# Row sums of a graph-attention layer: neighbouring key tiles added up by accumulating transfers before the product

## The chip, the cores and the metric

The kernel runs on one core of one Trainium2 chip. The metric is the device time of one execution in microseconds (us), from start to end of the program on that core; the number to forecast is the median over runs. Lower is better. In the text PE is the matrix engine (TensorE), DVE is VectorE, ACT is ScalarE, POOL is GpSimd, and SP is the engine that issues the plain DMAs.

## What is computed

Two attention layers over a graph of N = 2048 nodes, D = 256 features, for a batch of B = 8. Both end in a residual add and a layer norm:

```python
# layer 0: H = 8 heads of dh = 32
x_proj = einsum('bnd,hdf->bhnf', x, W)
e = leaky_relu(e_src[..., :, None] + e_dst[..., None, :], 0.2)
e = e + softplus(beta) * log(prior + 1e-6)      # prior = adj
e = where(adj > 0, e, -inf)
h = softmax(e, axis=-1) @ x_proj                # per head
x = layernorm(x + concat_heads(h) @ W_out.T)
# layer 1: one head of 256
e = where(adj > 0, leaky_relu((x @ W1) @ (x @ W2).T, 0.2), -1e12)
x = layernorm(x + relu(softmax(e, axis=-1) @ (x @ W3)))
```

The change sits in layer 0. There the kernel never forms a softmax. It uses that exp(leaky_relu(u + v)) can be written as a row factor times exp(v) times max(c, r), where c depends on the query and r on the key. So for a key tile of 128 keys and all 2048 queries it forms s = max(c, r) * m, with m the transposed edge weights. Two sums over the keys follow: the numerator, s times (exp(v) * x_proj), and the row sum (the softmax's denominator), s times exp(v). Both are matrix products with s as the moving operand.

## The kernel before

**Layer 0, class `Gat`, one object per batch element.** `project` makes the projected values `v` (already multiplied by exp) and `re`, which holds for each key and head r (`re[:, 0]`) and exp(v) (`re[:, 1]`). For elements 1 to 7 both are parked in DRAM (`v_d`, `re_d`) and fetched again by `load`.

`step` does one key tile for two heads. An element has 64 steps: an outer loop over 4 pairs of heads (`hp`), an inner one over 16 key tiles (`jt`). One step

- fetches the key tile's edge weights, 1 MB, into `mt` (L177, two buffers, issued by SP);
- makes one `s` tile of 128 x 2048 float32 for each of the two heads on DVE (L301). `s` has four buffers, which is two steps' worth;
- multiplies on PE (L309): first eight products into `val` (the numerator), then eight into `den` (the row sums). For `den` the stationary operand is exp(v) of the key tile, broadcast to 32 columns, so that every one of 32 output rows holds the same sum. Both accumulate in PSUM over the 16 key tiles.

After the last key tile `finish` copies `val` and `den` out on ACT (L323, L325), takes the reciprocals by way of DRAM (`rc`, `rec_d`) and, after every second pair of heads, fetches them as a broadcast tile `rb` (L336) and scales the numerator (L338). `rb` lives in the two buffers of the tag "d". In elements 1 to 7 nothing else uses that tag; the setup in element 0 does.

**Layer 1, class `Dot`.** For each of 16 query tiles: scores on PE (`e`, L402), a leaky relu out of PSUM on ACT (`p`, L404), the mask and row minimum on DVE (L407), exp on ACT (L408), then transposes on PE (`pt`, L421) that ACT copies out (`pts`, L423), and the product `acc` (L437). The scores of the next query tile are computed inside the step of the present one.

**How the two are laid beside each other.** The instruction order on PE is the order of the program text (`manual_schedule` for PE); the other engines' order is worked out by the framework's scheduler, and each engine then executes in order. The main loop runs layer 1 of element b-1 and layer 0 of element b together: one `Gat` step after every fourth tile of `output`, one after every second tile of `turn`, and then, in each `Dot.step`, zero to two steps at each of the three places where `fill` is called:

```python
        dot.step(lambda k: layer_0((2, 1, 1)[k]))
        for i in range(NT - 2):
            dot.step(lambda k: layer_0((0, 2 - (i % 2 == 1), 2 - (i % 14 == 13))[k]))
```

Element 0's layer 0 runs alone at the start (with the projections of the other elements between its steps), element 7's layer 1 alone at the end.

Of the kernel before, what the change touches and what calls it, by code (L numbers as in the profile page):

```python
# [9 lines left out]
F32 = mybir.dt.float32  # L10
BF16 = mybir.dt.bfloat16
I32 = mybir.dt.int32
AF = mybir.ActivationFunctionType
ALU = mybir.AluOpType
# [4 lines left out]
P = 128  # L19
# [8 lines left out]
def kernel(  # L28
# [26 lines left out]
    nc = tc.nc  # L55
    B, N, D = x.shape
    H, _, DH = w_proj.shape
    NT = N // P
    KC = D // P
    BK = 512  # L60
    NB = N // BK
    HALF = N // 2
    HP = 2
    NP = H // HP
    IG = BK // P

    const = ctx.enter_context(tc.tile_pool(name="const", bufs=1))
    dram = ctx.enter_context(tc.tile_pool(name="dram", bufs=1, space=DRAM))
# [3 lines left out]
    small = ctx.enter_context(tc.tile_pool(name="small", bufs=3))  # L72
# [3 lines left out]
    def mm_tile(name):  # L76
        return ps.tile([P, BK], F32, tag="mm", name=name)

    def wide_tile(name, tag, bufs, dtype=F32):
        return wide.tile([P, N], dtype, tag=tag, name=name, bufs=bufs)  # L80
# [69 lines left out]
    pen_d = dram.tile([N, N], BF16, name="pen_d")  # L150
    c_d = dram.tile([B, H, N], F32, name="c_d")
    v_d = dram.tile([B, P, NT, D], F32, name="v_d")
    re_d = dram.tile([B, P, 2, NT, H], F32, name="re_d")
    rec_d = dram.tile([B, NP, 4, HALF], F32, name="rec_d")
    x1_d = dram.tile([B, N, D], F32, name="x1_d")

    def make_mt(jt):

        a = wide.tile([P, NT, P], I32, tag="d", name="adj_t", bufs=2)
        nc.sync.dma_start(a, adj[:, ts(jt, P)].rearrange("(t p) j -> p t j", p=P))  # L160
        m = wide.tile([P, NT, P], F32, tag="p", name="m", bufs=2)
        nc.vector.tensor_scalar(m, a, 0.0, None, ALU.max)
        nc.scalar.activation(m, m, AF.Ln, bias=eps_prior)
        nc.scalar.activation(m, m, AF.Exp, scale=beta_c)
        nc.vector.scalar_tensor_tensor(m, a, 0.0, m, ALU.is_gt, ALU.mult)
        mt = wide_tile("mt", "mt", 2)
        for g in range(NB):
            t = mm_tile("mtp")
            for k in range(IG):
                nc.tensor.transpose(t[:, ts(k, P)], m[:, g * IG + k, :], ident)  # L170
            nc.scalar.copy(mt[:, ts(g, BK)], t)
        nc.sync.dma_start(mt_d[ts(jt, P), :], mt)
        return mt

    def load_mt(jt):
        mt = wide_tile("mt", "mt", 2)
        nc.sync.dma_start(mt, mt_d[ts(jt, P), :])  # L177
        return mt
# [21 lines left out]
    def row_tile(name, bufs=4):  # L200
        return small.tile([P, D], F32, tag="row", name=name, bufs=bufs)


    class Gat:
# [8 lines left out]
        def project(self):  # L213


            b = self.b
            kept = "v" if b == 0 else ("h3", "x1t")[b % 2]
            self.v = v = whole.tile([P, NT, D], F32, tag=kept, name="v")
            ed = small.tile([P, NT, H], F32, name="ed", bufs=1)
            es = small.tile([P, H, NT], F32, name="es", bufs=1)  # L220
            xb = x[b].rearrange("(t p) d -> p t d", p=P)
            xrs, xts = [], []

            def turn(g):
                if g % 2 == 0:
                    xr = wide.tile([P, 2 * IG, D], F32, tag="p", name="xr", bufs=2)
                    nc.sync.dma_start(xr, xb[:, ts(g // 2, 2 * IG), :])
                    xrs.append(xr)
                xt = chunk.tile([P, KC, BK], F32, tag="ht", name="xt", bufs=3)
                for kc in range(KC):  # L230
                    t = mm_tile("tr")
                    for k in range(IG):
                        nc.tensor.transpose(t[:, ts(k, P)], xrs[-1][:, g % 2 * IG + k, ts(kc, P)], ident)
                    nc.scalar.copy(xt[:, kc, :], t)  # L234
                xts.append(xt)

            turn(0)
            for g in range(NB):
                if g + 1 < NB:
                    turn(g + 1)  # L240
                for k in range(IG):
                    it = g * IG + k
                    t = mm_tile("proj")
                    for kc in range(KC):
                        nc.tensor.matmul(t[:, 0:D + 2 * H], xts[g][:, kc, ts(k, P)], wp[:, kc, :],  # L245
                                         start=(kc == 0), stop=(kc == KC - 1))
                    nc.scalar.copy(v[:, it, :], t[:, 0:D])
                    nc.scalar.copy(ed[:, it, :], t[:, D:D + H])
                    nc.scalar.copy(es[:, :, it], t[:, D + H:D + 2 * H])
                yield  # L250
            top = small.tile([P, 2, H], F32, name="top", bufs=1)
            nc.vector.tensor_reduce(top[:, 0, :], ed.rearrange("p t h -> p h t"), AX.X, ALU.max)
            nc.gpsimd.partition_all_reduce(top[:, 1, :], top[:, 0, :], P, bass_isa.ReduceOp.max)
            nc.vector.tensor_tensor(es, es, top[:, 1, :].unsqueeze(2).to_broadcast([P, H, NT]), ALU.add)
            nc.vector.tensor_tensor(ed, ed, top[:, 1:2, :].to_broadcast([P, NT, H]), ALU.subtract)
            self.re = re = small.tile([P, 2, NT, H], F32, name="re", bufs=2)
            nc.scalar.activation(re[:, 0], ed, AF.Exp, scale=-(1.0 - ALPHA))
            nc.scalar.activation(re[:, 1], ed, AF.Exp)
            v4 = v.rearrange("p t (h f) -> p (t h) f", f=DH)
            nc.vector.tensor_tensor(v4, v4, re[:, 1].rearrange("p t h -> p (t h)").unsqueeze(2).to_broadcast(  # L260
                [P, NT * H, DH]), ALU.mult)
            if b > 0:
                nc.sync.dma_start(v_d[b], v)
                nc.sync.dma_start(re_d[b], re)
            yield
            t = mm_tile("est")
            nc.tensor.transpose(t[:, 0:P], es.rearrange("p h t -> p (h t)"), ident)
            est = row_tile("est")[:, 0:P]
            nc.scalar.activation(est, t[:, 0:P], AF.Exp, scale=1.0 - ALPHA)
            nc.sync.dma_start(c_d[b].rearrange("h (t p) -> (h t) p", p=P), est)  # L270
            yield

        def load(self):
            self.v = whole.tile([P, NT, D], F32, name="v")
            nc.sync.dma_start(self.v, v_d[self.b])
            self.re = small.tile([P, 2, NT, H], F32, name="re", bufs=2)
            nc.sync.dma_start(self.re, re_d[self.b])

        def query_rows(self, h):
# [5 lines left out]
        def step(self, count=1):  # L285

            for _ in range(count):
                hp, jt = next(self.units)
                if jt == 0:
                    self.cs = [self.query_rows(hp * HP + a) for a in range(HP)]  # L290
                    self.val = pacc.tile([P, HALF], F32, tag="val", name="val")
                    self.den = pacc.tile([P, HALF], F32, tag="den", name="den")
                first = self.b == 0 and hp == 0
                while first and len(self.mts) < min(jt + 2, NT):
                    self.mts.append(make_mt(len(self.mts)))
                mt = self.mts[jt] if first else load_mt(jt)
                s = []
                for a in range(HP):
                    h = hp * HP + a
                    sa = wide_tile("s", "s", 4)  # L300
                    nc.vector.scalar_tensor_tensor(sa, self.cs[a], self.re[:, 0, jt, h:h + 1], mt, ALU.max, ALU.mult)  # L301
                    s.append(sa)
                for dst in (self.val, self.den):
                    for c in range(HALF // BK):
                        for q in range(4):
                            h = hp * HP + q % 2
                            w = (self.v[:, jt, ts(h, DH)] if dst is self.val
                                 else self.re[:, 1, jt, h:h + 1].to_broadcast([P, DH]))
                            nc.tensor.matmul(dst[ts(q, DH), ts(c, BK)], w,  # L309
                                             s[q % 2][:, ds(q // 2 * HALF + c * BK, BK)],  # L310
                                             start=(jt == 0), stop=(jt == NT - 1))
                if jt == NT - 1:
                    self.finish(hp)

        def finish(self, hp):

# [202 lines left out]
```

## Time and profile before

| | |
|---|---|
| median of 3 runs | 4691.11 us (4690.69 to 4692.31) |
| the profiled execution | 4692.34 us, of which the span from first to last instruction is 4690.5 us |
| mean granted PE clock | 0.982 |
| ACT busy | 1678.8 us (36%) |
| POOL busy | 4.5 us, 14 instructions |
| bytes moved by DMA | 852.27 MB, mean 182 GB/s |

Busy time of the engines in three stretches of the span:

| stretch, us | PE | DVE | ACT | DMA share |
|---|---|---|---|---|
| 117 to 234 (element 0) | 92.62 of 117 | 93.45 | 66.77 | 0.79 |
| 936 to 1053 (layer 0 beside layer 1) | 117.00 of 117 | 79.04 | 39.40 | 0.51 |
| 4446 to 4563 (layer 1 alone) | 117.00 of 117 | 24.49 | 59.65 | 0.15 |

The DMA share is the mean busy share of the core's 16 DMA engines. An engine's idle time is put down to the one that released it.

### The profile page before, as it was taken

The numbers are of one execution on the slowest core, as the hardware profiler recorded it, in microseconds if no ns is written. First come the engines' busy times: TensorE is split into PE (matmuls) and PEld (weight loads), VectorE is DVE, ScalarE is ACT, GpSimd is POOL, SyncE is SP. The second block draws the span as 40 slices with busy tenths as digits, with TensorE's granted clock in tenths as the row PEclk, the third lists the DMA queues.
The fourth block names the chain that finished last, engine by engine and source line by source line (L and its number), as shares of the span: only waits on it lengthen the run. The fifth ranks groups of instructions, "written<-read, shape, count | busy, mean of one in ns | idle before, by whom it ended". The sixth has DMA issues, their size and how long they took to land.

```text
span 4690.5 us, 64746 instructions
## 1 busy us (share of the span) xinstructions
PE 4474.0 (95%) x27164; PEld 2280.4 (49%) x27164; DVE 3048.5 (65%) x2316; ACT 1678.8 (36%) x3683; POOL 4.5 (0%) x14
## 2 busy tenths in 40 slices
PE   6798799998999989998999989999999989999899
PEld 4443344444444444444444444445454444444566
DVE  5787676666666666666766666666766666666221
ACT  6522133333333333333333333333333343333555
POOL 0000000000000000000000000000000000000000
PEclk9999899999999999999999999999999999999999
DMA  7788854555555454555544455555545555544111
GB/s 220 264 298 329 294 201 156 179 176 201 181 180 179 171 181 171 178 180 190 189 175 163 173 202 175 176 177 187 183 162 176 179 189 185 177 165 153 61 48 44
DMA packets 252789, 852.27 MB, mean 182 GB/s; under 512 B 33616, under 2 KB 152400, under 8 KB 174928
## 3 DMA queue, kind: packets, MB, share of 16 engines
q1 hardware_dynamic: 252496, 848.13, 52.0%
q8 instruction: 213, 3.49, 0.3%
q14 instruction: 80, 0.66, 0.0%
HBM read 772.15 MB, written 75.37 MB: 181 GB/s over the span
## 4 chain that ended last, share of the span: by engine, by line
PE 86%; DMA 2%; ACT 1%; DVE 1%; issue 0%; SPq 0%; DVEq 0%
PE e L402 19%; PE acc L437 19%; PE val L309 18%; PE den L309 17%; PE pt L421 5%; PE y L351 3%; PE h3p L371 2%; PE h1p L391 2%; DMA rb<-rec_d 1%; PE tr L366 1%; DVE s L301 0%; DVE ht L338 0%; DMA mt<-mt_d 0%; PE proj L245 0%; DMA rec_d<-rc 0%
## 5 line engine op out<-in xcount | busy, mean ns | idle before, releaser
L301 DVE SCALAR_TENSOR_TENSOR s<-c,re,mt 128x2048 f32<-128x2048 f32 x1024 | 2350.2, 2347 | 441.5 <-PE den L309 375.4
L309 PE MATMUL val<-s,v 128*32 128x512 f32 x8192 | 1018.7, 603 | 54.4 <-DVE s L301 54.3
L309 PE MATMUL den<-s,re 128*32 128x512 f32 x8192 | 995.2, 594 | 0.0
L437 PE MATMUL acc<-h,pts 128*128 128x256 f32 x4096 | 951.7, 380 | 14.7 <-ACT pts L423 14.7
L402 PE MATMUL e<-x1t,h 128*128 128x512 f32 x2048 | 904.3, 594 | 0.0
L437 PEld LDWEIGHTS acc<-h,pts 128*128 128x128 f32 x4096 | 750.4, 191 | 103.2 <-ACT pts L423 16.6
L407 DVE CUSTOM_DVE_ANT_0 p<-p,pen 128x2048 f32<-128x2048 f32 x128 | 293.4, 2292 | 482.4 <-ACT p L404 482.4
L423 ACT COPY pts<-pt 128x512 f32<-128x512 f32 x512 | 298.0, 584 | 841.6 <-PE pt L421 841.3
L402 PEld LDWEIGHTS e<-x1t,h 128*128 128x128 f32 x2048 | 379.7, 190 | 450.2 <-issue 424.6
L309 PEld LDWEIGHTS den<-s,re 128*32 128x32 f32 x8192 | 272.2, 110 | 617.8 <-issue 617.8
L309 PEld LDWEIGHTS val<-s,v 128*32 128x32 f32 x8192 | 235.3, 110 | 651.2 <-issue 544.8
L404 ACT ACTIVATE p<-e 128x512 f32<-128x512 f32 x512 | 305.6, 597 | 543.6 <-PE e L402 543.6
L445 DVE TENSOR_TENSOR z<-z,x1r 128x256 f32<-128x256 f32 x128 | 54.4, 425 | 463.6 <-ACT z L444 458.0
L408 ACT ACTIVATE p<-p,neg 128x2048 f32<-128x2048 f32 x128 | 256.7, 2005 | 267.6 <-DVE neg L407 267.6
L421 PEld LDWEIGHTS pt<-ident,p 128*128 128x128 f32 x2048 | 238.1, 141 | 223.3 <-issue 189.8
L421 PE MATMUL pt<-ident,p 128*128 128x128 f32 x2048 | 318.5, 279 | 5.2 <-ACT p L408 5.2
L351 PE MATMUL y<-wot,ht 128*128 128x256 f32 x512 | 140.5, 425 | 85.1 <-DVE ht L338 84.3
L444 ACT ACTIVATE z<-acc,rec 128x256 f32<-128x256 f32 x128 | 60.9, 476 | 356.6 <-PE acc L437 356.6
L194 ACT ACTIVATE f<-mv,eps_ln 128x1 f32<-128x1 f32 x256 | 74.5, 291 | 294.9 <-DVE mv L192 294.6
L351 PEld LDWEIGHTS y<-wot,ht 128*128 128x128 f32 x512 | 103.7, 211 | 129.7 <-DVE ht L338 87.5
L371 PE MATMUL h3p<-w3s,x1t 128*128 128x256 f32 x512 | 133.5, 386 | 7.3 <-ACT x1t L367 7.3
L245 PE MATMUL proj<-wp,xt 128*128 128x272 f32 x512 | 126.1, 397 | 1.5 <-ACT xt L234 0.7
(76 smaller groups left out, 1797.4 us busy)
## 6 DMA issues: line engine op xcount, KB each, us to landing
mt<-mt_d SPq DMA_DIRECT2D x496, 1024.0 KB, 4.8
c<-c_d SPq DMA_DIRECT2D x64, 1024.0 KB, 5.9
pen<-pen_d SPq DMA_DIRECT2D x128, 512.0 KB, 3.3
xr<-in_x_dram SPq DMA_DIRECT2D x16, 1024.0 KB, 8.5
adj_t<-in_adj_dram SPq DMA_DIRECT2D x16, 1024.0 KB, 7.2
mt_d<-mt SPq DMA_DIRECT2D x16, 1024.0 KB, 5.7
adj_r<-in_adj_dram SPq DMA_DIRECT2D x16, 1024.0 KB, 8.1
rb<-rec_d SPq DMA_DIRECT2D x64, 256.0 KB, 4.8
```

The costliest lines, as they stand in the source:

```text
L245: nc.tensor.matmul(t[:, 0:D + 2 * H], xts[g][:, kc, ts(k, P)], wp[:, kc, :], start=(kc == 0), stop=(kc == KC - 1))
L301: nc.vector.scalar_tensor_tensor(sa, self.cs[a], self.re[:, 0, jt, h:h + 1], mt, ALU.max, ALU.mult)
L309: nc.tensor.matmul(dst[ts(q, DH), ts(c, BK)], w, s[q % 2][:, ds(q // 2 * HALF + c * BK, BK)], start=(jt == 0), stop=(jt == NT - 1))
L351: nc.tensor.matmul(y[:, 0:D], ht[:, ts(it, P)], wot[:, g, :], start=(g == 0), stop=(g == 1))
L371: nc.tensor.matmul(t[:, 0:D], x1t[:, kc, ts(it - 1, P)], w3s[:, kc, :], start=(kc == 0), stop=(kc == KC - 1))
L402: nc.tensor.matmul(t, self.h1[:, kc, ts(it % IG, P)], self.x1t[:, kc, ts(c, BK)], start=(kc == 0), stop=(kc == KC - 1))
L404: nc.scalar.activation(p[:, ts(c, BK)], t, AF.Prelu, alpha=ALPHA)
L407: nc.vector.tensor_tensor_reduce(p, p, pen, -1.0, FMAX, ALU.add, ALU.min, neg)
L408: nc.scalar.activation(p, p, AF.Exp, bias=neg, scale=-1.0, accum_out=den)
L421: nc.tensor.transpose(t[:, ts(k, P)], p[:, ts(g * IG + k, P)], ident)
L423: nc.scalar.copy(pt, t)
L437: nc.tensor.matmul(acc, now[:, ts(k, P)], self.h3[:, j, :], start=(j == 0), stop=(j == NT - 1))
```

## The change

For elements 1 to 7, and for four pairs of neighbouring key tiles of every head, (1, 2), (5, 6), (9, 10) and (13, 14), the row-sum products of the two tiles become one. The first tile's s is multiplied, key by key, by the ratio exp(v of the first) / exp(v of the second); the result `d` is a new tile in the tag "d". The second tile's s is then added onto `d` by a DMA that accumulates, issued from POOL. One set of eight products with the second tile's exp(v) as weights gives the row sums of both. It is placed after the products of the key tile that comes two later (three after the pair's first); for the last pair, after tile 15. The numerator's products stay as they are. The ratios are a third plane of `re`, made in `project`.

```diff
@@ -63,6 +63,7 @@
+    PAIRED = (1, 5, 9, 13)
@@ -150,7 +151,7 @@
-    re_d = dram.tile([B, P, 2, NT, H], F32, name="re_d")
+    re_d = dram.tile([B, P, 3, NT, H], F32, name="re_d")
@@ -253,9 +254,13 @@
-            self.re = re = small.tile([P, 2, NT, H], F32, name="re", bufs=2)
+            self.re = re = small.tile([P, 3, NT, H], F32, name="re", bufs=2)
             nc.scalar.activation(re[:, 0], ed, AF.Exp, scale=-(1.0 - ALPHA))
             nc.scalar.activation(re[:, 1], ed, AF.Exp)
+            for k, jt in enumerate(PAIRED):
+                nc.vector.tensor_tensor(ed[:, k, :], ed[:, jt, :], ed[:, jt + 1, :], ALU.subtract)
+            nc.vector.memset(re[:, 2], 0.0)
+            nc.scalar.activation(re[:, 2, 0:len(PAIRED)], ed[:, 0:len(PAIRED)], AF.Exp)
@@ -300,17 +305,32 @@
-                for dst in (self.val, self.den):
-                    for c in range(HALF // BK):
-                        for q in range(4):
-                            h = hp * HP + q % 2
-                            w = (self.v[:, jt, ts(h, DH)] if dst is self.val
-                                 else self.re[:, 1, jt, h:h + 1].to_broadcast([P, DH]))
-                            nc.tensor.matmul(dst[ts(q, DH), ts(c, BK)], w,
-                                             s[q % 2][:, ds(q // 2 * HALF + c * BK, BK)],
-                                             start=(jt == 0), stop=(jt == NT - 1))
+                v, e = self.v, self.re[:, 1]
+                heads = [hp * HP + a for a in range(HP)]
+                broadcast_e = [e[:, jt, h:h + 1].to_broadcast([P, DH]) for h in heads]
+                self.products(self.val, [v[:, jt, ts(h, DH)] for h in heads], s, jt == 0, jt == NT - 1)
+                if self.b > 0 and jt in PAIRED:
+                    k = PAIRED.index(jt)
+                    self.sums = [wide_tile("d", "d", 2) for _ in heads]
+                    for d, sa, h in zip(self.sums, s, heads):
+                        nc.scalar.activation(d, sa, AF.Copy, scale=self.re[:, 2, k, h:h + 1])
+                elif self.b > 0 and jt - 1 in PAIRED:
+                    for d, sa in zip(self.sums, s):
+                        nc.gpsimd.dma_start(d, sa, accum_op=ALU.add)
+                    self.sums_e = broadcast_e
+                else:
+                    self.products(self.den, broadcast_e, s, jt == 0, self.b == 0 and jt == NT - 1)
+                if self.b > 0 and (jt - 3 in PAIRED or jt == NT - 1):
+                    self.products(self.den, self.sums_e, self.sums, False, jt == NT - 1)
                 if jt == NT - 1:
                     self.finish(hp)
+
+        def products(self, dst, weights, s, start, stop):
+            for c in range(HALF // BK):
+                for q in range(4):
+                    nc.tensor.matmul(dst[ts(q, DH), ts(c, BK)], weights[q % 2],
+                                     s[q % 2][:, ds(q // 2 * HALF + c * BK, BK)],
+                                     start=start, stop=stop)
```

`load` takes the third plane of `re` with it in the same way.

More of the change, by code (lines that the diff above doesn't have):

```diff
@@ L275, in load @@
             nc.sync.dma_start(self.v, v_d[self.b])
-            self.re = small.tile([P, 2, NT, H], F32, name="re", bufs=2)
+            self.re = small.tile([P, 3, NT, H], F32, name="re", bufs=2)
             nc.sync.dma_start(self.re, re_d[self.b])
```

## The prediction

> **What bounds the kernel now.** I read the page's first part, then the chain that ended last, then the groups, and then one loop turn in the timeline.
>
> ```profile
> PE 4474.0 (95%) x27164; PEld 2280.4 (49%) x27164; DVE 3048.5 (65%) x2316; ACT 1678.8 (36%) x3683; POOL 4.5 (0%) x14
> ...
> PE 86%; DMA 2%; ACT 1%; DVE 1%; issue 0%; SPq 0%; DVEq 0%
> ...
> L301 DVE SCALAR_TENSOR_TENSOR s<-c,re,mt 128x2048 f32<-128x2048 f32 x1024 | 2350.2, 2347 | 441.5 <-PE den L309 375.4
> L309 PE MATMUL val<-s,v 128*32 128x512 f32 x8192 | 1018.7, 603 | 54.4 <-DVE s L301 54.3
> L309 PE MATMUL den<-s,re 128*32 128x512 f32 x8192 | 995.2, 594 | 0.0
> ...
> L408 ACT ACTIVATE p<-p,neg 128x2048 f32<-128x2048 f32 x128 | 256.7, 2005 | 267.6 <-DVE neg L407 267.6
> ...
> mt<-mt_d SPq DMA_DIRECT2D x496, 1024.0 KB, 4.8
> ```
>
> PE carries 86% of the chain and DVE 1%: the kernel is PE-bound. DVE, which makes `s`, is idle 375.4 us because PE has not yet released an `s` buffer; PE in turn waits only 54.3 us for `s`. So DVE runs two steps ahead, held by the four buffers. The timeline shows the rhythm:
>
> ```profile
> 2555.06 1.90 PE L309 MATMUL val<-s,v 128*32 128x512 f32 x16
> 2556.78 1.90 PE L309 MATMUL den<-s,re 128*32 128x512 f32 x16
> ...
> 2559.10 7.03 PE L402 MATMUL e<-x1t,h 128*128 128x512 f32 x16
> 2566.06 1.92 PE L309 MATMUL val<-s,v 128*32 128x512 f32 x16
> ```
>
> ```profile
> 2555.29 9.14 DVE L301 SCALAR_TENSOR_TENSOR s<-c,re,mt 128x2048 f32<-128x2048 f32 x4 [1.97 <-PE den L309]
> ```
>
> A set of `val` or `den` products takes 1.72 us (2555.06 to 2556.78; the matmuls overlap, so starts are subtracted; the trace counts 16 instructions for eight calls). Two steps of `s` cost DVE 9.14 us, 2.3 us a tile, and start right after a `den` ends.
>
> **What the Trainium skill says.** "DMA: Bandwidth & Descriptors", § SWDGE vs HWDGE vs iDMA: a transfer that accumulates must be issued from GpSimd, whose software writes its descriptors. § Anatomy of one DMA of the same page gives about 2 us of fixed cost; § Bandwidth gives 6.15 us for a plain 1 MB load issued from GpSimd. The trace before has no such transfer; SP's 1 MB load lands in 4.8 us. "Collectives: The Full Stack", § The bandwidth ceiling, puts a DMA reduction at half the rate of a copy, because each result needs two source reads; no run here shows it yet. "SBUF — State Buffer", § Who interferes with whom: a two-input VectorE instruction disturbs GpSimd's reads, not its writes, so L301 should not hold up the descriptors (inferred there; not in this trace). "ScalarE: Activation LUTs", § What ACT_TABLE_LOAD costs: an ACTIVATE with one pointer operand on 2048 elements takes about 1990 ns; L408 agrees with 2005.
>
> **The change, part by part.**
>
> *Removed.* 7 elements x 4 head pairs x 4 tile pairs = 112 times, one set of `den` products goes (two out, one in): 112 x 1.72 = 193 us of PE, all on the path.
>
> *ACT.* 224 scaled copies at 2.0 us, 450 us, take ACT from 36% to about 46%: no bound. But ACT is in order, and behind a copy may stand a `pts` or `h1` copy that PE needs next. `pts` copies come every 2.2 us with some 1.4 us to spare (copied at 2575.93 + 0.59, PE done with the preceding `acc` at about 2577.6), and the copies of one pair become ready 2.3 us apart, at DVE's pace. Most delays hide. I take 0.3 us a pair, 34 us, plus 20 us for places where `h1` stands behind (a quarter of the turns). Bounds: 0 and 112 x 2 = 224 us.
>
> *The accumulating transfers.* 224 of 1 MB. Their price T is the unknown. The trace's DMA share of 0.51 in a 117 us stretch at 179 GB/s gives 0.51 x 117 / 20.9 MB = 2.85 us of all engines per MB of plain load. Lower end: SBUF is quicker than DRAM, and twice the reads hide partly, 4.2 us. Twice the plain price is 5.7. Upper end: the page's 6.15 us plus another read of 2.85, 9.0. I take 7.0, near the middle of 5.7 and 9.0. All 16 engines then carry 224 x 7.0 = 1570 us more, about 40% of the 3800 us in which they run, on top of 50%.
>
> *The wait added.* The second tile's `s` buffers are now free only when the transfer has landed, not when PE is done. Call four steps A (scaled), B (accumulated), C, D. D's `s` goes into B's buffers. From B's first `s` to the next B's first `s` stand: about 1 us of descriptors (an estimate: half the fixed cost), 2 T for both heads' transfers, which share the engines, 1 us of landing, 2.9 us for one `mt` load interleaved, and four more `s` tiles (D's second one, both of A', the first of B'), 9.2 us. Sum 14.1 + 2 T + 1 us for the semaphore and the SP issue of `mt` = 15.1 + 2 T. Up to 3.5 us of L407 and layer norm work on DVE falls into the same loop when it can't use the gap; I take half, 1.7 us. With T = 7.0: 29.1, or 30.8 us.
>
> PE's own cadence for four steps: a turn of `Dot` is 26.4 us with three steps and 29.8 us with four (2540 to 2596), so four steps take 32.1, less 1.72 = 30.4 us. The loop is 0.4 us longer than PE, and since steps are bunched I take 0.8 us, 91 times (13 of 16 pairs in an element): 73 us. In `turn`, with a step every 5.9 us, four steps take 23.6 - 1.7 = 21.9 us while the loop takes 29.1: 7.2 us, two cycles x 7 elements: 101 us. Behind the waiting `s` on DVE stand L407 and the layer norm, with slack of over ten us; behind it on SP stands the next `mt`, which waits for that `s` and holds `pen` and `x1r` behind it.
>
> *Late ends.* Pair (13, 14) is used one step later, at tile 15: 2 T + 5 = 19 us against 19 to 22 us of cover (the `val` set of tile 14, 1.7, tile 15, 3.4, a stretch of `Dot` between them, 7.9, and DVE's lead over PE, 6 to 9 by the timeline); 0.5 us x 28 = 14 us.
>
> *The tag "d".* `rb` and `d` share two buffers. After the second head pair the chain from the `ht` copy to L338's end takes 25 us (2455.5 to 2480.5), during which the next pair's second `d` can't start: some 17 us late, of which the slack leaves 4 us, x 7 = 28 us. At an element's end two of the four `rb` loads, so far issued early, come late: 1.5 us x 8 = 12 us. PE is already idle there for 10 us.
>
> *`project`, `re`.* Four small subtractions, a memset, one exp at 0.3 us per element, a transfer half as large again, hidden under element 0's layer 0 but for the first: 1 us.
>
> **Sum.** -193 + 54 + 73 + 101 + 14 + 40 + 1 = +90 us on the profiled 4692.3 us: 4782 us. The median of the runs is 1 us below the profiled execution: 4781. I say 4780.
>
> **Rivals.**
> *Faster: the buffers come back in time.* If T is 4.5 us the loop is 24.1 to 25.8 us, well under 30.4. Then `Dot` costs nothing, `turn` 2.2 x 14 = 31 us, the rest about 65: -193 + 96 = -97, 4594 us. For it: DVE's 375 us of waiting for PE and half the DMA time are free. Against it: the transfer must read two tiles in little more than 1.5 times a plain load's time. It turns into a loss at about T = 5.9, where stalls of some 83 us in `turn` stand beside 109 elsewhere.
> *Much slower: the transfer is three plain loads or more.* At T = 9.0 the loop takes 34.8 us: 4.4 x 91 = 400, `turn` 11.2 x 14 = 157, the rest 150, sum +514: 5206 us. At T = 12, some 1200 us more than before. For it: no view shows the accumulate rate; against it: DMA engines would sit near full load.
> *Nothing moves:* gain and stalls cancel within 9 us, 4691.
> *Another order on ACT:* if the scheduler puts the scaled copies ahead of `pts` and they wait for `s`, PE pays up to 2 us a pair: +170 us over the forecast, inside the slow cases.
>
> **How the numbers follow.** Slower as forecast (T 6 to 8): 0.44, own range 4705 to 4990. Much slower: 0.14. Faster: 0.37, own range 4560 to 4680. No change: 0.05. A range for 8 in 10 must reach into both sides: 4575 (leaving the best of the faster case) to 5210 (leaving the worst of the slowest). A measurement of this kernel tells 0.2%, some 9 us, from no change: faster 0.37, same 0.05, slower 0.58.
>
> **What would show it.** In the changed profile: `den` with 8192 - 1792 = 6400 instructions (112 x 16 gone) and, if my reason holds, a large idle time ahead of L301 put down to the accumulating DMA, and PE waiting for `s` far above 54 us, most at tiles 4 and 8, in `turn`. The transfers' time to landing, for two at once, would be 15 us or more. If they land within 10 us, L301 keeps waiting for PE alone and the forecast is wrong towards 4600. If PE instead waits for `pts` or `h1`, it was ACT's order. A longer wait at L351 would show the `rb` buffers.

## The result: 4829.9 us, and the profile after

The changed kernel takes 4829.93 us (median; 4826.25 to 4832.87), against 4691.71 us for the kernel before on the same chip: a ratio of 1.0288, 95% interval 1.0271 to 1.0306. It is 138 us slower. The profiled execution took 4826.25 us, its span 4824.4.

The page of the changed kernel, in the same order as before: the engines, the DMA queues, the costliest groups, the DMA issues.

```profile
PE 4424.8 (92%) x25372; PEld 2263.8 (47%) x25372; DVE 3052.6 (63%) x2356; ACT 2086.7 (43%) x3915; POOL 197.9 (4%) x238
...
q1 hardware_dynamic: 252496, 849.05, 48.7%
q0 software_dynamic: 32256, 234.90, 25.4%
...
L306 DVE SCALAR_TENSOR_TENSOR s<-c,re,mt 128x2048 f32<-128x2048 f32 x1024 | 2356.8, 2347 | 713.9 <-DMA mt<-mt_d 229.5
L331 PE MATMUL val<-s,v 128*32 128x512 f32 x8192 | 1063.1, 612 | 115.1 <-DVE s L306 114.9
...
L331 PE MATMUL den<-s,re 128*32 128x512 f32 x4608 | 615.7, 606 | 0.0
...
L316 ACT ACTIVATE d<-s,re 128x2048 f32<-128x2048 f32 x224 | 444.9, 2001 | 289.0 <-PE den L331 261.6
...
L331 PE MATMUL den<-d,re 128*32 128x512 f32 x1792 | 271.8, 643 | 69.8 <-DMA d<-s 69.8
...
mt<-mt_d SPq DMA_DIRECT2D x496, 1024.0 KB, 6.3
d<-s POOLq DMA_DIRECT2D x224, 1024.0 KB, 11.8
c<-c_d SPq DMA_DIRECT2D x64, 1024.0 KB, 15.3
```

`den` has 4608 + 1792 = 6400 instructions: the change does what it says. PE has 1792 instructions fewer, yet its busy time fell by only 49 us, and its idle time rose from 216.5 to 399.6 us. L306 is the old L301. One of its instructions takes 2347 ns in both kernels, so DVE itself has not become slower. Its idle time went from 441.5 to 713.9 us, and what ends the largest part of it is no longer PE but the landing of `mt`. A load of `mt` lands after 6.3 us instead of 4.8, and one of `c` after 15.3 us; before, `c` took 5.9.

The waits of DVE, the same view for both kernels (engine and line, what it waited for: us in total, times, longest). Before:

```profile
DVE s L301 <- PE den L309: 375.4, 281, 2.8
...
DVE s L301 <- DMA mt<-mt_d: 46.9, 22, 6.7
```

After:

```profile
DVE s L306 <- DMA mt<-mt_d: 229.5, 114, 7.4
...
DVE s L306 <- DMA d<-s: 135.8, 45, 6.2
DVE s L306 <- DMA c<-c_d: 126.2, 23, 6.7
...
DVE s L306 <- PE den L331: 114.0, 82, 4.1
```

DVE's lead over PE, the 375 us in which it waited for PE, has shrunk to 114. In its place stand three DMAs. Only one of them, `d<-s`, is the held buffer of the forecast (136 us); the two others are old loads that have become slow (356 us together, against 51 before).

By stage, from the starts of the `y` products and the end of the last `h3p` (PE's timeline of both kernels): the stretches with the scores took 456.4 us an element before and 469.5 after (mean of seven); `output` and `turn` took 86 us in elements 1 to 6 before and 87 to 93 after. So most of the loss, 7 x 13.1 = 92 us, lies beside the scores, and only some 23 us in those six `turn` stretches.

### The profile page after: what moved, and what is told of

Its sections match the earlier page's. It is cut to its first block, busy times and chain, and to the rows that moved or that the text cites. A ratio compares the mean times of both kernels' runs of the same rounds, so it can differ in the third digit from the quotient of the medians.

```text
span 4824.4 us, 62388 instructions
## 1 busy us (share of the span) xinstructions
PE 4424.8 (92%) x25372; PEld 2263.8 (47%) x25372; DVE 3052.6 (63%) x2356; ACT 2086.7 (43%) x3915; POOL 197.9 (4%) x238
## 3 DMA queue, kind: packets, MB, share of 16 engines
q0 software_dynamic: 32256, 234.90, 25.4%
## 5 line engine op out<-in xcount | busy, mean ns | idle before, releaser
L306 DVE SCALAR_TENSOR_TENSOR s<-c,re,mt 128x2048 f32<-128x2048 f32 x1024 | 2356.8, 2347 | 713.9 <-DMA mt<-mt_d 229.5
L331 PE MATMUL val<-s,v 128*32 128x512 f32 x8192 | 1063.1, 612 | 115.1 <-DVE s L306 114.9
L457 PE MATMUL acc<-h,pts 128*128 128x256 f32 x4096 | 972.8, 386 | 55.9 <-ACT pts L443 55.6
L422 PE MATMUL e<-x1t,h 128*128 128x512 f32 x2048 | 914.7, 598 | 15.7 <-ACT pts L443 9.8
L457 PEld LDWEIGHTS acc<-h,pts 128*128 128x128 f32 x4096 | 760.8, 193 | 157.7 <-ACT pts L443 66.7
L331 PE MATMUL den<-s,re 128*32 128x512 f32 x4608 | 615.7, 606 | 0.0
L316 ACT ACTIVATE d<-s,re 128x2048 f32<-128x2048 f32 x224 | 444.9, 2001 | 289.0 <-PE den L331 261.6
L319 POOL DMA_DIRECT2D d<-s x224 | 193.5, 864 | 3727.8 <-ACT d L316 1979.1
L331 PEld LDWEIGHTS den<-s,re 128*32 128x32 f32 x4608 | 169.2, 113 | 362.0 <-issue 360.2
L331 PE MATMUL den<-d,re 128*32 128x512 f32 x1792 | 271.8, 643 | 69.8 <-DMA d<-s 69.8
L371 PE MATMUL y<-wot,ht 128*128 128x256 f32 x512 | 137.4, 424 | 70.8 <-DVE ht L358 70.7
## 6 DMA issues: line engine op xcount, KB each, us to landing
d<-s POOLq DMA_DIRECT2D x224, 1024.0 KB, 11.8
c<-c_d SPq DMA_DIRECT2D x64, 1024.0 KB, 15.3
```

The source lines that it names most:

```text
L316: nc.scalar.activation(d, sa, AF.Copy, scale=self.re[:, 2, k, h:h + 1])
L319: nc.gpsimd.dma_start(d, sa, accum_op=ALU.add)
L331: nc.tensor.matmul(dst[ts(q, DH), ts(c, BK)], weights[q % 2], s[q % 2][:, ds(q // 2 * HALF + c * BK, BK)], start=start, stop=stop)
L371: nc.tensor.matmul(y[:, 0:D], ht[:, ts(it, P)], wot[:, g, :], start=(g == 0), stop=(g == 1))
L422: nc.tensor.matmul(t, self.h1[:, kc, ts(it % IG, P)], self.x1t[:, kc, ts(c, BK)], start=(kc == 0), stop=(kc == KC - 1))
L457: nc.tensor.matmul(acc, now[:, ts(k, P)], self.h3[:, j, :], start=(j == 0), stop=(j == NT - 1))
```

## The experiments

The theory on record was that the transfer holds the second tile's `s` buffers and so makes DVE late. Rivals: contention (the transfers' traffic slows the loads of `mt` and `c`), and ACT (the copies stand in front of others). The kernel before was timed again beside each of the four groups of runs: 4690.9, 4691.2, 4694.8 and 4692.7 us.

**PE alone.** The scaled copy, the transfer and the late product are gone; the second tile alone goes into `den`.

```diff
                 if self.b > 0 and jt in PAIRED:
+                    pass
                 elif self.b > 0 and jt - 1 in PAIRED:
+                    self.products(self.den, broadcast_e, s, False, False)
...
-                if self.b > 0 and (jt - 3 in PAIRED or jt == NT - 1):
-                    self.products(self.den, self.sums_e, self.sums, False, jt == NT - 1)
```

> Leaves out the 112 row-sum product sets of the scaled tiles, with no scaled copy and no transfer (the row sums lack those tiles). It prices the PE term alone. If the term is right: 4692 - 193 = about 4500 us. If PE is not what sets the end, clearly less is gained: above 4570.

Measured: 4514.3 us, ratio 0.9623 (0.9609 to 0.9638). The products removed are worth 177 us of the 193 counted.

**Copies without transfers.**

```diff
-                    for d, sa in zip(self.sums, s):
-                        nc.gpsimd.dma_start(d, sa, accum_op=ALU.add)
                     self.sums_e = broadcast_e
```

> Keeps the scaled copies on ACT, the buffers of d and the late product, leaves out the accumulating transfer (the row sums lack the second tile of each pair). Theory 'the s buffers are held by the transfer' and rival 'DMA contention': 4500 to 4570, the copies are nearly free. Rival 'ACT': the copies stand ahead of pts and h1 and wait for d; it stays above 4680.

Measured: 4536.3 us, 0.967 (0.9655 to 0.9684). The copies cost 22 us over PE alone. ACT waits here nearly as long for `d` to be released as in the changed kernel:

```profile
ACT d L316 <- PE den L329: 240.6, 84, 5.6
```

In the changed kernel this wait is 261.6 us. It is long, and it stands at the head of an in-order engine, yet without transfers a wait like it costs at most the 22 us. The rival "ACT" falls as a cause of its own. That ACT's order hands on delays which the transfers cause is another matter, and is seen below.

**Transfers that hold no `s`.**

```diff
-                        nc.gpsimd.dma_start(d, sa, accum_op=ALU.add)
+                        nc.gpsimd.dma_start(d, v[:, 0:8, :].rearrange("p t d -> p (t d)"), accum_op=ALU.add)
```

> The transfers stay, same size and number and same destination, but read the values tile v, so that s is not held (the row sums are wrong in the second tiles). Theory 'the s buffers are held': most of the loss goes, 4560 to 4650. Rival 'DMA contention', the loads of mt and c are slowed by the traffic: 4760 to 4830, nearly as with the change.

The transfer reads 2048 elements a partition of `v` in place of the second tile's `s`. Measured: 4757.5 us, 1.0134 (1.0114 to 1.0153), just under the band of the rival. Of the 294 us between "copies without transfers" and the changed kernel, 72 go with the hold on `s`; 221 stay. The theory on record explains a quarter of the loss. Two reserves: these transfers needn't wait for the second tile, so they start earlier than the real ones, and PE still waits 69.0 us for `d`, so the 221 us are not contention alone.

**Traffic that PE doesn't wait for.** Each `d` is written twice to DRAM in place of the accumulation; PE's product waits only for the copy. The next copy into `d` must wait until the writes have landed; the trace has one such wait on ACT, 7.2 us.

```diff
-                    for d, sa in zip(self.sums, s):
-                        nc.gpsimd.dma_start(d, sa, accum_op=ALU.add)
+                    for a, d in enumerate(self.sums):
+                        for r in range(2):
+                            nc.gpsimd.dma_start(scr[(jt // 4 % 4) * 4 + 2 * a + r], d)
```

> The scaled copies and the late product stay; instead of the accumulating transfer each d is written twice to a scratch area in DRAM (from GpSimd, plain, 2 MB a head and pair; the row sums lack the second tiles). Nobody on PE waits for it and it holds no s. Theory 'contention: traffic delays the loads of mt and c and with them DVE': 4680 to 4790, most of what e3_other_source lost. Rival 'it is the waits for d and its two buffers': within 60 us of e2_no_transfer, 4530 to 4600.

Measured: 4713.9 us, 1.0044 (1.0027 to 1.0061): 178 us above "copies without transfers", inside the band of contention. The DMA queues show that the load on the engines is the same as that of the accumulations (25.4% of 16 engines there):

```profile
q0 software_dynamic: 64512, 469.79, 25.1%
```

and DVE waits for the same two loads:

```profile
DVE s L307 <- DMA mt<-mt_d: 223.3, 106, 7.8
...
DVE s L307 <- DMA c<-c_d: 89.0, 29, 4.4
```

The way from there to PE shows in the waits of PE and of ACT in this run:

```profile
PE y L373 <- DVE ht L360: 119.1, 8, 20.5
PE val L333 <- DVE s L307: 75.0, 40, 9.8
PE acc L459 <- ACT pts L445: 52.6, 15, 7.3
PE e L424 <- ACT p L426: 34.2, 7, 5.2
```

```profile
ACT d L317 <- DVE s L307: 95.8, 15, 8.1
```

Without transfers the same waits of PE were:

```profile
PE val L329 <- DVE s L306: 79.3, 37, 11.2
PE y L369 <- DVE ht L356: 59.3, 8, 20.1
...
PE acc L455 <- ACT pts L441: 7.4, 15, 0.6
```

PE's direct wait for `s` has not grown. Three others have: for `y` by 60 us, for `pts` by 45 and for `p` by 34 (without transfers none is listed). Together they are the growth of PE's idle time, from 223.8 to 360.7 us; the rest of the 178 us is PE's own work, 35 us longer at the same number of instructions. The timeline of ACT and DVE shows how `pts` and `p` become late: at the first steps of a head pair `c` and then `mt` land late and make a late `s`, ACT's scaled copy waits for it (up to 8.1 us), and the `pts` or `p` copy behind it on ACT comes late for PE. For `y`, the `rc` and `rb` transfers at an element's end are slower (8.6 and 5.4 us to landing, against 2.6 and 4.5).

The changed kernel divides the loss in another way:

```profile
PE val L331 <- DVE s L306: 114.9, 57, 9.8
PE y L371 <- DVE ht L358: 70.7, 8, 20.1
PE den L331 <- DMA d<-s: 69.8, 15, 5.8
PE acc L457 <- ACT pts L443: 55.6, 21, 5.5
...
PE e L422 <- ACT pts L443: 9.8, 12, 2.5
```

Against the run without transfers PE waits 70 us more for `d`, 58 for `pts`, 36 for `s` and 11 for `y`. That is its added idle time of 176 us. Its busy time is 114 us longer for the same 25372 instructions (4310.8 to 4424.8). So little of DVE's lateness reaches PE as a wait for `s`.

**How the loss grows with the bytes.** The second tile is added only in a quarter, or half, of the columns.

```diff
-                        nc.gpsimd.dma_start(d, sa, accum_op=ALU.add)
+                        nc.gpsimd.dma_start(d[:, 0:BK], sa[:, 0:BK], accum_op=ALU.add)
```

> The change with transfers of a quarter of the columns (512 of 2048; the row sums lack the rest of the second tiles): same number of transfers, same waits, a quarter of the bytes. Theory 'bytes' (held buffers and contention both grow with them): 4540 to 4600. Rival 'the fixed path' (GpSimd's descriptors, the landing, the semaphores): above 4700.

> Transfers of half of the columns (the row sums lack the other half of the second tiles). A quarter cost nothing. If the loss starts only where the transfer outgrows the slack of mt's load and of the s buffers: 4545 to 4610. If it grows evenly from a quarter to the whole: 4535 + 295 / 3 = about 4630.

Measured: a quarter 4534.6 us, half 4570.8 us, the whole 4829.9 us. From none to the whole: 4536, 4535, 4571, 4830. The first quarter is free, the second costs 36 us, the second half 259. The 224 issues on GpSimd, their descriptors and semaphores cost nothing that shows; the loss is one of bytes. `mt` lands after 4.8, 5.1, 5.7 and 6.3 us in these four, and `c` after 5.9, 8.0, 10.3 and 15.3. That the loss begins where the slack of these loads ends is a reading: the hold on `s` grows with the bytes too.

**The last pair earlier.** All pairs move one tile forward, and `den` starts at tile 2.

```diff
-    PAIRED = (1, 5, 9, 13)
+    PAIRED = (0, 4, 8, 12)
```

> The change with the pairs one tile earlier, (0,1), (4,5), (8,9), (12,13), so that the last pair too has two tiles between its transfer and its product. Theory 'a part of the loss is the late last pair': 70 us of waits for d and as many lost clock cycles go, 4690 to 4750. Rival 'contention and held buffers alone': 4800 to 4840, no change.

Measured: 4811.7 us, 1.0262 (1.0245 to 1.0278), 18 us better than the change and inside the rival's band. PE's wait for `d` has all but gone (4.1 us), and so has DVE's for `c`, but DVE now waits 218.8 us for held `s` buffers (135.8) and PE 83.6 us for `pts` (55.6). Taking away one late end moved the wait.

**Half as many pairs.**

```diff
-    PAIRED = (1, 5, 9, 13)
+    PAIRED = (4, 10)
```

> Two pairs a head instead of four, (4,5) and (10,11), six tiles apart, neither at the end. PE loses half of its 177 us of work. Theory 'loss where transfers meet short cadence and late ends': stalls well under half of the change's, 4620 to 4670. Rival 'loss proportional to the bytes': half the change's effect, about 4760.

Measured: 4704.2 us, 1.0028 (1.0017 to 1.0039). If half of the pairs bring half of the PE gain, 88 us, and half of the cost of the copies, 11, then the two pairs lost some 90 us through their transfers, against 294 for four. That is between the two theories. Fewer pairs of the whole size didn't pay here: DVE waited 279.9 us for `mt`, longest 11.0, so even transfers that lie far apart seem to catch a load of `mt`.

**The sum on DVE instead.** One instruction per head makes `d` from both tiles.

```diff
-                        nc.scalar.activation(d, sa, AF.Copy, scale=self.re[:, 2, k, h:h + 1])
...
+                    for d, sa, sb, h in zip(self.sums, self.first, s, heads):
+                        nc.vector.scalar_tensor_tensor(d, sa, self.re[:, 2, k, h:h + 1], sb, ALU.mult, ALU.add)
```

> Same arithmetic as the change, but one DVE instruction per head makes scaled first tile plus second tile: no ACT copy, no transfer; 224 x 2.35 = 526 us more on DVE, the sums product one step after the pair. If PE stays the bound: 4500 plus 30 to 90 for turn, where four steps need 23.1 us of DVE against 21.9 of PE: 4530 to 4590. Rival: DVE falls behind also beside the scores: above 4692.

> The sum made on DVE (as in e4_dve_add) for the two pairs (4,5) and (10,11) only: 263 us more on DVE. If DVE's lead is rebuilt between the pairs: 4600 to 4660. Rival, every added DVE instruction costs as in e4_dve_add (214 us above the PE-only run for 224 of them): half of that, about 4710.

Measured: four pairs 4728.1 us, 1.0074 (1.0056 to 1.0092); two pairs (4 and 10) 4641.2 us, 0.9893 (0.9878 to 0.9908). With four, DVE is 75% busy and PE waits for it:

```profile
PE val L330 <- DVE s L306: 192.4, 115, 11.2
```

With two it is 69.9 us. Here too the first half is cheap (38 us above what half of PE's gain would give) and the second dear (214 us for four); the two pairs also lie at other tiles than the four.

**Half and half.** Both resources have some slack that is free, so the right half of the columns goes to DVE and the left half to ACT and the transfer; then 768 columns by transfer and 1280 by DVE.

```diff
-                        nc.scalar.activation(d, sa, AF.Copy, scale=self.re[:, 2, k, h:h + 1])
+                        nc.scalar.activation(d[:, 0:HALF], sa[:, 0:HALF], AF.Copy, scale=self.re[:, 2, k, h:h + 1])
...
+                        nc.gpsimd.dma_start(d[:, 0:HALF], sb[:, 0:HALF], accum_op=ALU.add)
+                        nc.vector.scalar_tensor_tensor(d[:, HALF:], sa[:, HALF:], self.re[:, 2, k, h:h + 1], sb[:, HALF:],
+                                                       ALU.mult, ALU.add)
```

> Same arithmetic as the change: the left half of the columns by scaled copy and accumulating transfer, the right half by one DVE instruction (1.2 us a head). 263 us more on DVE as in f4_dve_two (38 us lost there), half the bytes. If the two costs add: g1_half plus 40, 4580 to 4650, faster than the kernel before. Rival: later loads and more work meet on DVE: above 4690.

> As g2_hybrid with 768 of 2048 columns by transfer and 1280 by DVE: 66 us more on DVE, a quarter less traffic. If the transfers still cost more than the DVE work at a half (g1_half stood 35 us above the quarter): 4570 to 4590. If DVE is now the dearer of the two: 4595 to 4630. Equal: the two are balanced near the half.

Measured: 4593.3 us, 0.9786 (0.9771 to 0.98), and 4600.6 us, 0.9803 (0.979 to 0.9817). Both beat the kernel before by about 2% with the full arithmetic of the change; the two splits can't be told apart. The half split, in the same view as above:

```profile
PE 4333.9 (94%) x25372; PEld 2237.1 (49%) x25372; DVE 3319.8 (72%) x2580; ACT 1909.9 (42%) x3915; POOL 197.4 (4%) x238
...
L306 DVE SCALAR_TENSOR_TENSOR s<-c,re,mt 128x2048 f32<-128x2048 f32 x1024 | 2358.6, 2346 | 347.8 <-PE den L335 173.1
```

What most delays an `s` tile is PE again, as in the kernel before. PE's wait for `s`, 122.8 us, is its largest wait here.

More buffers for `s` or `d`, the direct way to take the hold away, were not run. So the 72 us of the hold rest on one run with another source.

## Why the prediction was right, point by point

The forecast was 4780 us and slower; it came out slower, 50 us beyond, inside the range. The direction had the right reason in part only: the transfers do make DVE late, but mainly by another way than the one priced, and the nearness of the number is luck. Taken away one after the other, the parts are 4691 - 177 (PE) + 22 (copies) + 221 (transfers without a hold on `s`) + 72 (the hold), which is 4830 but for rounding; another order might divide them otherwise.

- *Removed, 193 us.* Measured 177. Where the other 16 us went was not followed up.
- *ACT, 54 us.* Measured 22 without transfers. With them PE's waits for `pts` grew by 58 us. In the timeline some stand behind a scaled copy (at 764 and 1323 us), others behind a layer norm that DVE had delayed (at 1133 and 1695 us). The spare time of `pts` was also misread: its two times give 1.1 us, not 1.4.
- *The tag "d".* I saw that `rb` and `d` share two buffers and priced 40 us. PE's wait at L371 is 70.7 us (84.3 before, 59.3 without transfers), so little of that shows. I overlooked that the next pair's copy must wait for the late product on `d`; that is the long wait on ACT, nearly free in the run without transfers.
- *The price T, 7.0 us.* The term was mis-sized. From the page of the changed kernel, 0.254 x 4824.4 us / 224 = 5.47 us of all engines for one transfer of 1024 KB. A plain load of the same size costs 3.0 by my own figure, because the 2.85 us stand for 10^6 bytes and a transfer has 1.049 million. So an accumulation costs 1.8 plain loads, near my lower anchor of two and near the half rate that the Trainium skill's "Collectives: The Full Stack", § The bandwidth ceiling, puts down to two source reads; "DMA: Bandwidth & Descriptors", § Bandwidth, on which the upper anchor stood, was not needed.
- *The wait added, 73 + 101 us.* This is the step that failed. With T = 5.47 my loop is 26.0 to 27.7 us, under PE's 30.4 beside the scores: the scores would have cost nothing, `turn` 4.1 x 14 = 58 us, and my sum, -193 + 58 + 109, would have said 26 us faster. The hold measured 72 us. The place was wrong too: I put more than half into `turn`. Against the run without transfers the stretches with the scores are 33.0 us longer (436.5 to 469.5), 231 us in all, and the six `turn` stretches together 54.
- *What was missing: contention.* I counted 40% more DMA load and then let it cost one interleaved `mt` load, 2.9 us in a loop. Traffic alone, with no hold and no wait for `d` on PE, costs 178 us. I never asked how late `mt` and `c` may land. The page before had both sides of it for `mt`: 4.8 us to landing against 4.6 us of DVE work in a step, so that only DVE's waits for PE were left as slack.
- *Also missing: PE's own work.* 114 of the 290 us between the profiled executions of the run without transfers and of the changed kernel are longer busy time of PE at the same number of instructions; the last section has the part that the clock can account for.
- *Late ends, 14 us.* PE waited 69.8 us for `d`, but moving the pair gave back only 18.

The signs that I had named fell between the cases. A transfer lands after 11.8 us in the median (6.9 to 19.8): less than the 15 of the forecast, more than the 10 below which I would have been wrong. PE's wait for `s` rose from 54 to 115 us; of its growth over the run without transfers 23 of 36 us lie in `turn`, where I expected most.

So two errors, T too high and the other costs of traffic left out, partly cancelled. My rival "faster" had T = 4.5 and a turning point of 5.9. That point doesn't come out of my loop: 83 us over 14 cycles are a wait of 5.9 us, and 15.1 + 2 T = 21.9 + 5.9 gives T = 6.4. T came below either and the kernel was slower all the same. That is what the missing terms did.

## What to carry to other kernels

A transfer moved onto free DMA engines is not free while its traffic meets a load with little slack of its own: compare the load's time to landing with the work that covers it, not the engines' mean share. Slack on a second engine and on the DMA queues is worth using in small parts: the first quarter of the bytes and the first half of the DVE work cost little here, and a split over both beat either alone. A large wait in the list says little until a run without its cause is made: in the run without transfers 241 us of waiting on ACT were worth 22 at most.

## What the hardware showed that I had not expected

In this kernel a long idle stretch of PE is paid for twice: once as idle time, and again as slower work after it. In the changed kernel PE waits 4.8 us for `d`; the timeline of PE and the windows around it (PE busy, weight loads, DVE, ACT, POOL, then the granted clock, the DMA share, GB/s):

```profile
1405.47 1.02 PE L331 MATMUL den<-d,re 128*32 128x512 f32 x2
1411.27 3.63 PE L331 MATMUL den<-d,re 128*32 128x512 f32 x14 [4.77 <-DMA d<-s]
```

```profile
1405.00:1410.00 5.00, 1.49 (x10) 0.22 (x2) 1.11 (x1) 2.48 (x4) 0.00 (x0) 0.99 0.99 264
1410.00:1415.00 5.00, 3.73 (x15) 0.75 (x16) 3.44 (x2) 0.02 (x1) 0.00 (x0) 0.50 0.98 410
1415.00:1420.00 5.00, 5.00 (x24) 4.43 (x25) 3.54 (x3) 4.06 (x4) 0.00 (x0) 0.82 0.64 214
1420.00:1425.00 5.00, 5.00 (x30) 3.65 (x32) 0.61 (x2) 1.06 (x2) 0.00 (x0) 1.00 0.76 238
```

After the wait the clock is at half for some 5 us: 14 instructions take 3.63 us where 16 take 1.90. Slow work follows all fourteen waits for `d` of 3.9 to 5.8 us: the 14 instructions behind them take 3.28 to 3.64 us. Over the whole span, span x (1 - mean clock) is 4824.4 x 0.037 = 179 us, against 4534.6 x 0.018 = 82 us in the run with copies and no transfers: about 97 us of the 290 between these two executions (an estimate from rounded means). That would be most of the 114 us by which PE's busy time differs there; the rest stays unexplained, and the ends of matmuls are modelled.

The other surprise is how near an accumulation comes to two plain writes: one of 1024 KB takes the engines 5.47 us, and two writes of that size to DRAM 2 x 2.64 (0.251 x 4706.7 / 448). Beside the same kernel they cost 221 us (without the hold on `s`, but with PE waiting 69 us for `d`) and 178 us.
